# Gradient products of a trained layer: the derivative as stationary operand, tokens with a column of ones as moving operand

## The chip, the cores and the metric

The kernel runs on one core of one Trainium2 chip. The metric is the device time of one execution in microseconds; the kernel before takes 12997.07 us (median of three runs, 12996.37 to 12998.29).

## The reference, cut to what matters

Four layers follow each other on x of shape (8, 64, 64, 64): a selective-scan block with attention-like gates, a channel and position attention, a layer whose weights are trained inside the forward pass, and a second attention. Only the third is touched:

```python
def _modifier(params, x):
    w1, gn_w, gn_b, w2 = params
    h = jnp.einsum('bchw,oc->bohw', x, w1)          # 64 -> 128 channels
    ...                                             # group norm over 8 groups, per image
    h = _gelu(h)                                    # exact gelu
    return jnp.einsum('bohw,co->bchw', h, w2)       # 128 -> 64 channels
...
loss_fn = lambda ps: _surprise(_modifier(ps, feat) + feat, running_mean, running_var)
for _ in range(INNER_STEPS - 1):                    # two steps
    grads = jax.grad(loss_fn)(params)
    moms = ...
    params = ...
```

An image has 64 x 64 = 4096 tokens. For the gradients the kernel needs, for each image: the product of the output's derivative dy with the activations (64 x 128, summed over all images it is the gradient of w2), the product of the derivative t before the gelu with the tokens (128 x 64), and the sum of t over the tokens (128 numbers). From the last two it works out the gradients of w1 and of the norm's gain and bias.

## The kernel before

`modifier_and_attention` (L1803) builds a `Modifier`, calls `moments` once (L1819), and then twice `prepare`, `slope`, `gradients`, `update` (L1821 to L1825). `moments` (L1356) loads the images in pairs, subtracts each channel's mean and keeps the tokens transposed in `xT`, 128 tokens on the partitions, for every image and each of 32 groups of 128 tokens 64 channels. `slope` computes dy for all tokens.

`gradients` (L1535) is the stage of the change. It works on blocks of 512 tokens of a pair of images, eight blocks for a pair, four pairs, so 32 blocks in a pass. For a block n:

- `hidden` (L1553): eight products of 128 tokens each into two PSUM banks (L1562); ScalarE squares them, adds a tiny number and copies them (L1566, L1567, L1570).
- `factors` (L1576): ScalarE's gelu into `at` (L1580) and exponential into `t` (L1581), each after a load of its activation table[...].
- `remainder` (L1583), `invert` (L1591), `derive` (L1595): VectorE makes `half` (L1587) and, for each image, a reciprocal (L1593); GpSimd makes from them the gelu's derivative with three operations per image (L1596 to L1598).
- `back` (L1600): TensorE brings dy back through w2 and also transposes it, 192 columns, the two images in the upper and lower half of the array's rows (L1609).
- `keep_dy` (L1614): ScalarE copies the transposed dy out of PSUM (L1617).
- `apply` (L1619): VectorE multiplies the derivative with what came back (L1623). GpSimd adds the result to a running sum `run` over the blocks of the pair (L1629 for the first block, L1631 for the others).
- `sums` (L1633): for each of the four groups of 128 tokens and each image two products: dy (stationary, 64 columns) with the activations (128 moving columns) into the rows 0 to 63 of the image's PSUM bank `acc` (L1642), and the tokens (stationary, 64 columns) with t (128 moving columns) into the rows 64 to 127 (L1645). They add up in PSUM over the eight blocks.
- `collect` (L1650), after the last block of a pair: four products of `run` with a column of ones for each image (L1656), copies out of PSUM, w2's gradient added by VectorE (L1662, L1664), and a transposition of the tokens' product (L1667), so that `mom` gets 128 rows of 64 columns and, in column 64, the sum of t.

The order of all this is written by hand (L1670 to L1696, under `manual_schedule`), and every engine takes its instructions in that order. Iteration n issues `factors`, `invert` of image 0, `remainder` and `derive` of image 0 for block n + 1, `keep_dy` of n, `hidden` of n + 2, `apply` of n, `invert` and `derive` of image 1 for n + 1, `sums` of n, `back` of n + 1, and `collect` where a pair ends.

Buffers set who waits for whom. `at`, `t`, `e` and `h` have two buffers, so the gelu of block n + 2 waits until `sums` of block n has read `at`, and the exponential of n + 2 until all have read `t` of n. `half` and `dyT` have one. The PSUM banks of `hidden` are two, so its products for block n + 2 wait until VectorE has read those of n + 1 in `remainder`. The two pairs of banks of `back` are one block's, and `acc` has two banks, one for each image of the pair.

## Time and profile before

| | |
|---|---|
| median of three runs | 12997.07 us |
| the profiled execution | 12995.36 us |
| its span, first to last instruction | 12993.6 us |
| mean granted TensorE clock over the span | 0.926 |
| PE busy | 11161.9 us (86%) |
| DVE busy | 10881.6 us (84%) |
| ACT busy | 7717.6 us (59%) |
| POOL busy | 6754.4 us (52%) |
| first gradient pass, 9930 to 10300 us: PE, DVE, ACT, POOL busy | 254.28, 307.22, 286.15, 310.28 us |
| second pass, 10417 to 10785 us | 252.50, 306.03, 286.16, 310.25 us |

PE is TensorE's matmuls, PEld its weight loads, DVE VectorE, ACT ScalarE, POOL GpSimd. A line of the groups gives the source line, engine and operation, the tile written and those read, the shapes and the count; after the first bar the busy time and the mean duration in ns; after the second the idle time of the engine just before, with what ended it. A line of the waits gives who waited for whom, the sum in us, the times and the longest. A line of the windows gives the stretch in us from the span's start, its length, the busy time of each engine in it with the number of instructions, then the granted clock of TensorE as a share of full speed, and two numbers on DMA. The two gradient passes are some 700 us of the 12994; the rest is the scan, the attentions and the stages around them.

### The profile page before, as it was taken

Reading aid. Unit: us, or ns where it says so; the run is one execution under the profiler, and the core shown is the slowest. Engines: PE = TensorE matmul, PEld = TensorE weight load, DVE = VectorE, ACT = ScalarE, POOL = GpSimd, SP = SyncE. Lnnn points to the kernel's source line nnn. Section 1 sums busy time; section 2 is a strip of 40 time slices with the busy share of each in tenths; the row PEclk is TensorE's granted clock in tenths of the full one; section 3 lists DMA queues with packets and bytes.
Section 4 is the critical chain, followed back from the end, with each engine's and each line's share of the span. In section 5 each row is a group of like instructions: output and inputs, shape, how many; then the busy total and the mean of one; then the engine's idle time right before and its main releaser. Section 6 shows DMA issues by size and latency. Waiting matters only on the chain. (4 is left out here: it accounts for less than half of the span.)

```text
span 12993.6 us, 115955 instructions
## 1 busy us (share of the span) xinstructions
PE 11161.9 (86%) x36395; PEld 4115.1 (32%) x36395; DVE 10881.6 (84%) x7636; ACT 7717.6 (59%) x10047; POOL 6754.4 (52%) x3126
## 2 busy tenths in 40 slices
PE   7788888888888888888887779999996768999999
PEld 2233232232232232232232222323324553333332
DVE  5999999999999999999999958677686786766766
ACT  4676675675675666766765536445465674544544
POOL 4877888878888888788788830000003681000000
PEclk8999999999999999999999989999998888999999
DMA  4888888888889888888888830000001100000000
GB/s 164 301 292 291 308 301 293 306 298 303 300 300 309 296 296 308 300 298 305 297 299 304 295 120 6 24 18 11 17 6 66 39 27 23 6 16 17 6 10 6
DMA packets 686280, 2333.69 MB, mean 180 GB/s; under 512 B 98224, under 2 KB 98896, under 8 KB 683088
## 3 DMA queue, kind: packets, MB, share of 16 engines
q1 hardware_dynamic: 685648, 2326.13, 51.8%
q8 instruction: 290, 4.75, 0.1%
q14 instruction: 342, 2.80, 0.1%
HBM read 2240.69 MB, written 76.28 MB: 178 GB/s over the span
## 5 line engine op out<-in xcount | busy, mean ns | idle before, releaser
L614 POOL TENSOR_TENSOR ct<-ct,h 128x1024 f32<-128x1024 f32 x2048 | 4799.6, 2357 | 1447.1 <-DVE h L605 969.2
L642 PE MATMUL yps<-ct,ident 128*128 128x512 f32 x8192 | 4233.9, 652 | 547.3 <-POOL ct L614 545.3
L605 DVE TENSOR_TENSOR_SCAN h<-a,state,bdu 128x1024 f32<-128x1024 f32 x1344 | 3153.8, 2347 | 227.3 <-ACT state L609 26.7
L915 DVE TENSOR_TENSOR sum<-sum,ex 128x1024 f32<-128x1024 f32 x1920 | 2347.9, 1223 | 770.7 <-ACT ex L908 655.6
L908 ACT ACTIVATE ex<-sc 128x1024 f32<-128x1024 f32 x2048 | 1985.1, 1021 | 1529.8 <-PE sc L903 1529.7
L642 PEld LDWEIGHTS yps<-ct,ident 128*128 128x128 f32 x8192 | 1586.9, 205 | 3164.6 <-issue 1959.1
L582 ACT ACTIVATE a<-dt,amat 128x1024 f32<-128x1024 f32 x2048 | 2333.4, 1142 | 18.1 <-POOL dt L535 14.9
L601 DVE TENSOR_TENSOR bdu<-bt,du 128x1024 f32<-128x1024 f32 x1792 | 2194.9, 1225 | 101.4 <-ACT du L561 46.3
L922 PE MATMUL av<-ex,v 128*64 128x512 f32 x8192 | 1987.8, 606 | 0.0
L609 ACT COPY state<-h 128x1 f32<-128x1 f32 x2048 | 382.9, 187 | 2191.1 <-DVE h L605 2189.4
L903 PE MATMUL sc<-q,k 16*128 16x512 f32 (+1 forms) x8192 | 1656.3, 628 | 5.0 <-ACT ex L908 4.4
L605 DVE TENSOR_TENSOR_SCAN h<-a,bdu 128x1024 f32<-128x1024 f32 x448 | 1024.3, 2286 | 83.5 <-ACT state L609 16.7
L922 PEld LDWEIGHTS av<-ex,v 128*64 128x64 f32 x8192 | 498.2, 136 | 1363.9 <-issue 1360.5
L903 PEld LDWEIGHTS sc<-q,k 16*128 16x128 f32 (+1 forms) x8192 | 562.1, 184 | 1078.8 <-ACT ex L908 743.5
L1220 POOL TENSOR_TENSOR gt<-gt,pad 128x1024 f32<-128x1024 f32 x16 | 34.9, 2180 | 1617.5 <-ACT gt L1219 1538.1
L590 POOL TENSOR_TENSOR bt<-bt,dus 128x1024 f32<-128x1024 f32 x256 | 602.9, 2355 | 8.9 <-DMA bt<-bc 8.8
L408 PE MATMUL vps<-pad,convd 128*128 128x512 f32 x1152 | 534.2, 597 | 5.6 <-ACT z L393 5.6
L605 DVE TENSOR_TENSOR_SCAN h<-a,state,bt 128x1024 f32<-128x1024 f32 x192 | 499.5, 2602 | 15.0 <-POOL bt L590 8.2
L1593 DVE RECIPROCAL r<-e 128x512 f32<-128x512 f32 x128 | 420.7, 3323 | 0.0
L637 PE MATMUL yps<-y,ident 128*128 128x512 f32 x384 | 301.7, 917 | 115.6 <-ACT y L623 115.5
L1596 POOL TENSOR_TENSOR r<-r,half 128x512 f32<-128x512 f32 x128 | 162.7, 1271 | 360.9 <-issue 188.0
L582 ACT ACT_TABLE_LOAD x265 | 340.0, 1283 | 4.7
(402 smaller groups left out, 10325.1 us busy)
## 6 DMA issues: line engine op xcount, KB each, us to landing
bt<-bc SPq DMA_DIRECT2D x2048, 512.0 KB
ct<-bc SPq DMA_DIRECT2D x2048, 512.0 KB
x<-x SPq DMA_DIRECT2D x12, 2048.0 KB
bc<-e SPq DMA_DIRECT2D x256, 64.0 KB
zd<-z SPq DMA_DIRECT2D x64, 256.0 KB
z<-zd SPq DMA_DIRECT2D x64, 256.0 KB
x<-x SPq DMA_DIRECT2D x32, 512.0 KB
part<-x SPq DMA_DIRECT2D x128, 128.0 KB
```

The source lines that it names most:

```text
L408: nc.tensor.matmul(held[0].rearrange("p (r c) -> p r c", c=S), convd[:, t, :], pad[:, j * rows + dy : (j + 1) * rows + dy, dx : dx + S], s ...
L582: nc.scalar.activation(ctl["a", n], ctl["dt"], AF.Exp, scale=amat[:, ctl["k"], n : n + 1])
L590: nc.gpsimd.tensor_tensor(bt, bt, ctl["dus"], ALU.mult)
L601: nc.vector.tensor_tensor(z, bt, ctl["du"], ALU.mult)
L605: nc.vector.tensor_tensor_scan(h[:, flip], a[:, flip], z[:, flip], 0.0 if state is None else state[:, n : n + 1], ALU.mult, ALU.add,)
L614: nc.gpsimd.tensor_tensor(ct, ct, h, ALU.mult)
L642: nc.tensor.matmul(ctl["ps"][:, bass.ts(i, BK)], cm.ident, ct[:, bass.ts(i, BK)], start=False, stop=(n == N - 1),)
L903: nc.tensor.matmul(sc[:, e, :], k[r : r + d, bass.ts(j, 128)], qs[i][r : r + d, :], start=True, stop=True,)
L908: nc.scalar.activation(ex, sc, AF.Exp)
L915: nc.vector.tensor_tensor(sums[i], sums[i], ex, ALU.add)
L922: nc.tensor.matmul(avs[i][r, :], v[:, j, r], ex[:, e, :], start=(j == 0), stop=(j == TQ - 1))
L1593: nc.vector.reciprocal(r[n][s], e[n][:, s])
```

## The change

The token tile `xT` gets 65 columns instead of 64, the last of them filled with ones by VectorE. The second product of `sums` is turned round: t is the stationary operand (128 columns) and the tokens with their ones column move (65 columns), so that its result has 128 rows of 65 columns, in the orientation of `mom`, with the sum over the tokens in column 64. It now takes the columns 0 to 64 of the image's bank in all 128 rows; dy's product stands in the columns 128 to 255, image 0 in the rows 0 to 63, image 1 in the rows 64 to 127. Since the two products no longer share their start, each bank is opened with a product of zeros (one row, 128 columns stationary, 256 moving), and all others add to it. In each group of tokens the two dy products are issued first, then the two derivative products.

GpSimd's running sum goes, and with it in `collect` the products with the column of ones, the intermediate copies and the transpositions; ScalarE copies 128 x 65 numbers for each image. w2's gradient is gathered in a tile of 128 rows, one half for each image of the pair, and the halves are added after the last pair.

```diff
--- before.py
+++ after.py
@@ -1360,6 +1360,7 @@
         cm, nc, work = self.cm, self.cm.nc, self.work
         self.xc, self.pooled = self.kt([C + 1, NB, C], "xc"), self.kt([C, NB], "pooled")
         self.xT = tokens
+        self.cm.nc.vector.memset(tokens[:, :, :, C : C + 1], 1.0)
         cols = work.tile([2 * C, NB // 2], F32, name="mcols", tag="mcols")
         for p in range(NB // 2):
             x = self.load_pair(scratch[:, p, :], p, slice(0, L))
@@ -1381,7 +1382,7 @@
                         ps[:, i].rearrange("t b c -> t (b c)"), x[:, bass.ts(4 * j + i, 128)],
                         cm.ident,
                     )
-                dst = tokens[:, 2 * p : 2 * p + 2, 4 * j : 4 * j + 4, :]
+                dst = tokens[:, 2 * p : 2 * p + 2, 4 * j : 4 * j + 4, :C]
                 src = ps.rearrange("t q b c -> t b q c")
                 if j % 2:
                     nc.scalar.copy(dst, src)
@@ -1390,7 +1391,7 @@
             ps = self.bank("xxps")
             for q in range(TQ):
                 for e in range(2):
-                    t = tokens[:, 2 * p + e, q, :]
+                    t = tokens[:, 2 * p + e, q, :C]
                     nc.tensor.matmul(
                         ps[e * C : (e + 1) * C, :C], t, t, start=(q == 0), stop=(q == TQ - 1)
                     )
@@ -1539,7 +1540,10 @@
         cm, nc, work, p, g = self.cm, self.cm.nc, self.work, self.now, self.grad
         mom = self.kt([HID, NB, C + 1], "mom")
         blocks = [(pr, j) for pr in range(NB // 2) for j in range(NBK)]
-        at, t, h, e, r, half, hp, dyT, dp, acc, run = ({} for _ in range(11))
+        at, t, h, e, r, half, hp, dyT, dp, acc = ({} for _ in range(10))
+        w2 = work.tile([128, HID], F32, name="w2sum", tag="w2sum", bufs=1)
+        zero = work.tile([1, 2 * HID], F32, name="zero", tag="zero", bufs=1)
+        nc.vector.memset(zero, 0.0)
 
         def fetch(n):
 
@@ -1618,54 +1622,51 @@
 
         def apply(n):
 
-            pr, j = blocks[n]
             for s in range(2):
                 nc.vector.scalar_tensor_tensor(
                     t[n][:, s], t[n][:, s], 0.5, dp[n][s][:, :, :HID], ALU.add, ALU.mult
                 )
             dp.pop(n)
-            if j == 0:
-                run[pr] = work.tile([128, 2, 4, HID], F32, name="run", tag="run", bufs=1)
-                nc.gpsimd.tensor_copy(run[pr], t[n])
-            else:
-                nc.gpsimd.tensor_tensor(run[pr], run[pr], t[n], ALU.add)
 
         def sums(n):
+
 
             pr, j = blocks[n]
             if j == 0:
 
+
                 acc[pr] = [accs.tile([128, BK], F32, name="acc", tag="acc") for s in range(2)]
+                for ps in acc[pr]:
+                    nc.tensor.matmul(
+                        ps[:, : 2 * HID], zero[:, :HID], zero, start=True, stop=False
+                    )
             for i in range(4):
+                stop = j == NBK - 1 and i == 3
                 for s in range(2):
-                    flags = dict(start=(j == 0 and i == 0), stop=(j == NBK - 1 and i == 3))
                     nc.tensor.matmul(
-                        acc[pr][s][:C, :HID], dyT[n][:, s, i, :], at[n][:, s, i, :], **flags
-                    )
+                        acc[pr][s][s * C : (s + 1) * C, HID : 2 * HID], dyT[n][:, s, i, :],
+                        at[n][:, s, i, :], start=False, stop=False,
+                    )
+                for s in range(2):
                     nc.tensor.matmul(
-                        acc[pr][s][C:, :HID], self.xT[:, 2 * pr + s, 4 * j + i, :],
-                        t[n][:, s, i, :], **flags,
+                        acc[pr][s][:, : C + 1], t[n][:, s, i, :],
+                        self.xT[:, 2 * pr + s, 4 * j + i, :], start=False, stop=stop,
                     )
 
         def collect(pr):
 
-            momT = work.tile([128, 2, HID], F32, name="momT", tag="momT", bufs=1)
-            for s, ps in enumerate(acc[pr]):
-                b = 2 * pr + s
-                for i in range(4):
-                    nc.tensor.matmul(
-                        ps[:, HID : HID + 1], run[pr][:, s, i, :], cm.ones[:, 0:1],
-                        start=(i == 0), stop=(i == 3),
-                    )
-                nc.scalar.copy(momT[C:, s, :], ps[C:, :HID])
-                if b == 0:
-                    nc.vector.tensor_copy(g["w2"], ps[:C, :HID])
+            for s, ps in enumerate(acc.pop(pr)):
+                rows = slice(s * C, (s + 1) * C)
+                nc.scalar.copy(mom[:, 2 * pr + s, :], ps[:, : C + 1])
+                if pr == 0:
+                    nc.vector.tensor_copy(w2[rows], ps[rows, HID : 2 * HID])
                 else:
-                    nc.vector.tensor_tensor(g["w2"], g["w2"], ps[:C, :HID], ALU.add)
-                nc.scalar.copy(mom[:, b, C : C + 1], ps[:, HID : HID + 1])
-            for s, ps in enumerate(acc.pop(pr)):
-                nc.tensor.transpose(ps[:, 2 * HID : 2 * HID + C], momT[C:, s, :], cm.ident[C:, C:])
-                nc.scalar.copy(mom[:, 2 * pr + s, :C], ps[:, 2 * HID : 2 * HID + C])
+                    nc.vector.tensor_tensor(
+                        w2[rows], w2[rows], ps[rows, HID : 2 * HID], ALU.add
+                    )
+            if pr == NB // 2 - 1:
+                nc.vector.tensor_copy(g["w2"], w2[C:])
+                nc.vector.tensor_tensor(g["w2"], g["w2"], w2[:C], ALU.add)
 
         with self.cm.tc.manual_schedule():
             fetch(0)
@@ -1816,7 +1817,7 @@
             accs = train.enter_context(tc.tile_pool(name="t_acc", bufs=2, space=PSUM))
             mod.two = lambda: wide.tile([128, 2, BK], F32, name="hnps", tag="dps")
             ys = tok.tile([2 * C, NB // 2, L], F32, name="ys")
-            mod.moments(tok.tile([128, NB, TQ, C], F32, name="xT"), ys)
+            mod.moments(tok.tile([128, NB, TQ, C + 1], F32, name="xT"), ys)
             gs = mod.gates()
             for s in range(STEPS):
                 mod.prepare(wide)
```

## The prediction

> **What bounds the kernel now.** I read the page first (span, engines, slices), then the groups of the stretch 9900 to 10800 us, which holds both gradient passes, then the waits there, the timeline of a few blocks, and TensorE's clock in short windows.

> ```profile
> span 12993.6 us, 115955 instructions
> PEclk8999999999999999999999989999998888999999
> POOL 4877888878888888788788830000003681000000
> ```

> The page: slices 31 to 33 are the only ones in the second half in which GpSimd works and TensorE's granted clock drops; there lies the change. Groups of 9900 to 10800 us:

> ```profile
> L1593 DVE RECIPROCAL r<-e 128x512 f32<-128x512 f32 x128 | 420.7, 3323 | 0.0
> L1642 PE MATMUL acc<-at,dyT 128*64 128x128 f32 x1024 | 187.3, 344 | 9.5 <-ACT dyT L1617 9.5
> L1562 PE MATMUL htps<-hw,part 65*128 65x128 f32 x1024 | 186.8, 356 | 180.3 <-DVE half L1587 159.2 <-issue 21.1
> L1645 PE MATMUL acc<-t,xT 128*64 128x128 f32 x1024 | 180.4, 343 | 16.9 <-DVE t L1623 16.8
> L1596 POOL TENSOR_TENSOR r<-r,half 128x512 f32<-128x512 f32 x128 | 162.7, 1271 | 360.9 <-issue 188.0 <-DVE half L1587 163.5 <-DVE r L1593 9.3
> L1631 POOL TENSOR_TENSOR run<-run,t 128x1024 f32<-128x1024 f32 x56 | 132.3, 2363 | 1.6 <-DVE t L1623 1.6
> L1656 PE MATMUL acc<-ones,run 128*128 128x1 f32 x128 | 18.8, 277 | 1.6 <-POOL run L1631 1.6
> ```

> Each float32 product counts twice (x1024 for 64 blocks of 8). Waits of 9930 to 10800 us:

> ```profile
> ACT e L1566 <- PE htps L1562: 72.2, 58, 13.4
> DVE t L1623 <- ACT dyT L1617: 51.4, 38, 1.4
> ACT momT L1660 <- PE acc L1656: 32.2, 10, 8.4
> ACT L1580 <- PE acc L1645: 30.1, 30, 1.3
> ```

> In the timeline the first `half` (L1587) of a pass's block 0 and of its block 31 stand 327.7 us apart (9944.2, 10271.9; second pass 327.0): 31 intervals, 10.28 us each, or 13.3 where a `collect` lies in it. Per block GpSimd needs 10.16 (start to start of L1596, 10098.36 to 10108.52), VectorE 8.81 where it never idles (10094.80 to 10103.61), ScalarE 8.81. Two things hold the 10.28: GpSimd is full, and every second block TensorE is slow, so that ScalarE waits for it. The windows show the second:

> ```profile
> 10077.64:10081.05 3.41, 0.01 (x2) 0.00 (x0) 3.41 (x2) 3.37 (x4) 3.25 (x4) 1.00 0.00 0
> 10081.05:10084.47 3.42, 3.04 (x14) 3.04 (x15) 3.42 (x5) 1.97 (x5) 3.26 (x4) 0.50 0.00 0
> 10084.47:10087.88 3.41, 3.41 (x30) 3.19 (x31) 3.41 (x2) 2.69 (x5) 3.41 (x2) 0.50 0.36 81
> 10087.88:10091.29 3.41, 2.04 (x26) 1.57 (x22) 2.10 (x2) 2.76 (x3) 3.25 (x4) 1.00 0.00 1
> 10098.12:10101.53 3.41, 0.07 (x2) 0.00 (x0) 3.41 (x3) 3.37 (x4) 3.25 (x4) 1.00 0.00 0
> ```

> After the length come PE, PEld, DVE, ACT, POOL and the clock: an empty stretch of 3.41 us, then two at half clock, then full.

> **The change, part by part.** *Removed:* L1629/L1631, 140.6 us of GpSimd; it then needs about 8.0 a block and bounds nothing. Next is VectorE's 8.81.

> *TensorE's sums (L1642/L1645).* Before, the two products of an image sit side by side in 64 columns each: 16 steps of 0.109, 1.74 us. After, only the dyT products pair (8 steps, 0.87); the derivative is a 128-column weight, alone in the array, 16 steps that the load holds at 0.112 though only 65 columns move (1.79). And the mode changes 8 times within the sums instead of once, each 0.09 plus a slow second step of 0.05 to 0.10: 0.17, in all 1.36. Sums: 4.0 at full clock. The switch is the unknown: 0 if a load hides in it, 0.25 if it costs both slow steps in full; sums 2.7 to 4.7. At half clock 8 x 0.213 + 16 x 0.224 + 8 x 0.22 = 7.0.

> *The ring at full clock.* The next gelu into `at` waits for the last dyT product (release 0.24); then table and gelu 2.35, table and exponential 2.36, first dyT copy 0.31, two applies 1.28, and sums from the first derivative product to the last dyT one, 4.0 - 0.4 - 0.6 = 3.0: 9.5 us, over VectorE's 8.81. At half clock TensorE's own queue is longer: L1562 3.78 (the chain's pieces), sums 7.0, L1609 2.6, changes 0.2: 13.6.

> *Which clock.* At 9.5 TensorE works 1.9 + 4.0 + 1.5 and is idle 2.1. A window needs 0.38 x 3.413 = 1.30 us of streaming. One that holds the gap has 1.3 us of neighbours, L1609 (streams 1.28 in 1.5) and L1562 (65 rows count as 96: 1.28 in 1.9): at most 1.1. So it falls, as does one with 1.6 to 1.9 us of the gap; such windows begin over about 1.7 of the 3.41 us, one gap in two. Thin sums (1.7 streamed in 4.0) don't help. A half-clock block leaves no gap, and L1609 with L1562 behind it fills a window to 0.765, so it lasts about a block; the return comes at a window's end, often in the next block. Share f of half-clock blocks: from (1 - f)/2 = f a third, with the late return up to a half. I take 0.42: 0.58 x 9.5 + 0.42 x 13.6 = 11.2 a block.

> *Collect.* Before, 13.3 instead of 10.28, since L1656 waits for L1631 and ScalarE and VectorE for it. After, two copies of 65 columns (two of 0.22), two VectorE operations of 0.28 before the next reciprocal, and at the next block's start four steps of zero product of 256 columns (0.213, at half clock double): 0.9 to 1.7. I take 1.3, three times: 4.

> *End of a pass.* Before, 10271.9 to 10292.1. L1631 (2.35), L1656 (3.58 at half clock) and two transposes go; the derivative products after the last apply take about 6 instead of 3.2. Gain 2.5 (0 to 4).

> *Small.* Strided token copies (32 of 0.6), a memset of 256 columns, the zero memsets, two more operations on g["w2"]: between -1 and +2 us; I take 0. The scan and both attentions keep their instructions.

> *Sum.* A pass: 31 x 11.2 + 4 = 351.2 against 327.4: +23.8; less 2.5: +21.3. Twice: +43. The profiled execution took 12995.36 for a span of 12993.6; +43 is 13038, and the median lies 1.7 above it: 13040.

> **Rivals.** *The clock stays full.* Then 31 x 9.5 + 3 + 2 (cold start) = 299.5: -28, end -2.5, twice: 12936, faster. For it: GpSimd really is full before, and TensorE works more. Against: a gap of 2.1 cannot fill a window. It decides below f = 0.25. 13%. *The gap and the gain balance:* f = 0.25 gives 10.5 a block, 31 x 10.5 + 4 - 2.5 = 327: 12997; cheap switches (sums 2.7) end near here as well, as the ring falls to 8.9 but the gap grows to 2.7. 17%. *The clock locks at half:* 13.6 us is almost four windows (13.65), so a block may fall at the same place each time; f = 0.7: 12.4 a block, twice +57: 13112, or above. 9%. *The forecast,* f from 0.3 to 0.6, 13010 to 13085: 61%. That the sum does something else is excluded: column 64 of the product is the sum over tokens.

> **How the numbers follow.** About 0.2% (26 us) is what a measurement can tell from no change. Faster is the first rival and a little of the second: 0.15; same most of the second and the low end of the forecast: 0.19; slower 0.66. The range 12965 to 13110 leaves out the full-clock case and most of the lock.

> **What would show it.** Derivative products stepping 0.11 at full clock, sums near 4.0; blocks between 9.4 and 13.7 us in no fixed rhythm; mean clock near 0.75 over a pass's regular blocks (0.82 over 10036.68 to 10122.01 before); GpSimd idle 2 us a block; ScalarE's gelu waiting for the dyT products. Wrong if the windows stay at 1.00, if the sums take under 3 us, or if every block takes the same time.

## The result, and the profile after

| | before | after |
|---|---|---|
| median | 12996.72 us (4 runs, 12993.31 to 12998.29) | 13096.01 us (4 runs, 13084.72 to 13114.83) |
| profiled execution | 12995.36 us | 13114.83 us |
| first pass, `half` of block 0 to `half` of block 31 | 327.8 us | 388.6 us |
| second pass | 327.0 us | 387.9 us |
| last `half` to the next stage, each pass | 20.2, 20.2 us | 18.7, 19.7 us |
| mean clock in these two stretches | 0.81, 0.81 | 0.61, 0.61 |

The changed kernel is slower, by under one per cent but clear of noise: ratio 1.0080, 95% interval 1.0068 to 1.0092, 99 us by the medians. Its profiled execution is the longest of its four. The two loops account for all of the profiled pair's 119.5 us: 60.8 and 60.9 more, less 1.5 and 0.5 at their ends. The rest of the kernel is unchanged.

The page of the changed kernel, its span, TensorE's clock and GpSimd in 40 slices:

```profile
span 13113.1 us, 115634 instructions
POOL 4877888888888888888788710000004361000000
PEclk8999998999999999998999889999997668999999
```

In slices 31 to 34, which hold the gradient passes, GpSimd goes from 3, 6, 8 and 1 tenths to 4, 3, 6 and 1, and in slices 31 to 33 the clock from three times 8 to 7, 6 and 6. The groups of 9900 to 10900 us in the changed kernel (its L1597, L1566, L1646, L1651, L1600 are L1593, L1562, L1642, L1645, L1596 of before):

```profile
L1597 DVE RECIPROCAL r<-e 128x512 f32<-128x512 f32 x128 | 420.8, 3324 | 0.2
L1651 PE MATMUL acc<-xT,t 128*128 128x65 f32 x1024 | 256.9, 395 | 0.7 <-DVE t L1626 0.3
L1566 PE MATMUL htps<-hw,part 65*128 65x128 f32 x1024 | 209.0, 387 | 62.0 <-DVE half L1591 44.5 <-issue 17.5
L1600 POOL TENSOR_TENSOR r<-r,half 128x512 f32<-128x512 f32 x128 | 162.3, 1268 | 601.3 <-DVE half L1591 297.8 <-issue 184.0 <-DVE r L1597 119.5
L1646 PE MATMUL acc<-at,dyT 128*64 128x128 f32 x1024 | 161.7, 408 | 5.5 <-ACT dyT L1621 5.5
```

VectorE's and GpSimd's operations take what they took. L1566 is an instruction that the change doesn't touch, and yet its mean goes from 356 to 387 ns, and its idle time from 180.3 to 62.0 us: TensorE is slow more often and waits less. The waits of 9930 to 10860 us turn round accordingly:

```profile
ACT L1584 <- PE acc L1646: 160.4, 53, 5.4
DVE half L1591 <- ACT at L1584: 134.8, 41, 5.7
ACT e L1570 <- PE htps L1566: 70.1, 87, 14.4
ACT mom L1660 <- PE acc L1651: 17.8, 10, 5.5
```

Before, TensorE waited for `half`; now the gelu waits for TensorE's sums, 53 times in the 64 blocks, and VectorE for the gelu. In the traces of both kernels the granted clock is 1.00 or 0.50, and each record of it but the last lasts a whole number of 3.41 us (6.83, 10.24, 13.65 us and so on; 638 records before, 600 after). Ten windows of 3.41 us, in two stretches, show why it stays so (busy time of PE, PEld, DVE, ACT, POOL, then the clock):

```profile
10168.12:10171.54 3.42, 3.42 (x19) 2.98 (x18) 1.53 (x3) 3.39 (x5) 1.66 (x2) 0.50 0.00 0
10171.54:10174.95 3.41, 3.41 (x18) 2.86 (x17) 3.41 (x3) 2.48 (x4) 2.14 (x2) 0.50 0.13 38
10174.95:10178.36 3.41, 3.41 (x19) 2.51 (x18) 3.41 (x2) 1.12 (x3) 2.36 (x2) 0.50 0.15 38
10178.36:10181.78 3.42, 3.42 (x18) 2.85 (x19) 0.69 (x1) 2.31 (x2) 1.43 (x2) 0.50 0.00 0
10181.78:10185.19 3.41, 3.41 (x19) 2.97 (x18) 1.92 (x4) 2.99 (x5) 2.05 (x2) 0.50 0.00 0
...
10219.33:10222.74 3.41, 3.41 (x20) 3.12 (x20) 1.03 (x2) 3.38 (x3) 0.60 (x2) 0.50 0.00 0
10222.74:10226.15 3.41, 3.40 (x30) 2.74 (x28) 2.05 (x4) 3.37 (x7) 2.87 (x3) 1.00 0.16 32
10226.15:10229.57 3.42, 3.42 (x32) 2.70 (x34) 3.42 (x2) 2.93 (x5) 1.27 (x2) 1.00 0.13 44
10229.57:10232.98 3.41, 1.20 (x14) 0.91 (x11) 3.41 (x3) 3.37 (x4) 3.25 (x4) 1.00 0.00 0
10232.98:10236.39 3.41, 3.41 (x18) 3.19 (x19) 3.05 (x4) 2.26 (x6) 3.25 (x3) 0.50 0.10 24
```

At half clock PE is busy without a break, and VectorE and ScalarE have time to spare (in single windows they are busy for only 0.69 and 1.12 us). The clock stays at half for 68.27 us here (10154.47 to 10222.74), five blocks: one of 14.73, the first of a pair, and four of 13.27. It returns at 10222.74; the first gap, of 2.21 us, in the window at 10229.57, ends the full clock 10.24 us after the return. This pattern fills both passes: runs of one to five blocks at half clock, 13.27 us each (14.7 for the first of a pair), and between them a block of 10.33, often with one or two of 11.1 to 12.6, in which the clock changes. By the share that the prediction used (the part of a window in which TensorE streams, weighted by rows; that rows count in steps of 32 was the author's choice and is not shown), the windows at half clock from 10168.12 on read, in fours, one block or so to a row:

```
0.81 0.66 0.52 0.65
0.78 0.61 0.53 0.72
0.75 0.62 0.53 0.73
0.72 0.60 0.51 0.81 -> full clock
```

### The profile page after: what moved, and what is told of

Its sections match the earlier page's. It is cut to its first block, busy times and chain, and to the rows that moved or that the text cites. A ratio compares the mean times of both kernels' runs of the same rounds, so it can differ in the third digit from the quotient of the medians.

```text
span 13113.1 us, 115634 instructions
## 1 busy us (share of the span) xinstructions
PE 11427.6 (87%) x36283; PEld 4297.0 (33%) x36283; DVE 10887.3 (83%) x7643; ACT 7716.5 (59%) x10015; POOL 6618.2 (50%) x3062
## 3 DMA queue, kind: packets, MB, share of 16 engines
q1 hardware_dynamic: 685648, 2326.13, 51.4%
## 5 line engine op out<-in xcount | busy, mean ns | idle before, releaser
L605 DVE TENSOR_TENSOR_SCAN h<-a,state,bt 128x1024 f32<-128x1024 f32 x192 | 497.0, 2589 | 18.4 <-POOL bt L590 11.6
L1600 POOL TENSOR_TENSOR r<-r,half 128x512 f32<-128x512 f32 x128 | 162.3, 1268 | 601.3 <-DVE half L1591 297.8
L1597 DVE RECIPROCAL r<-e 128x512 f32<-128x512 f32 x128 | 420.8, 3324 | 0.2
```

The costliest lines, as they stand in the source:

```text
L605: nc.vector.tensor_tensor_scan(h[:, flip], a[:, flip], z[:, flip], 0.0 if state is None else state[:, n : n + 1], ALU.mult, ALU.add,)
L1597: nc.vector.reciprocal(r[n][s], e[n][:, s])
```

## The experiments

Theory A: the gap of 2.1 us makes the clock fall, the thin sums keep it from coming back, and TensorE at half clock is the bound. Thin are sums whose products stream for only a part of the time that they take, as the derivative products, where 65 columns move in a step of 0.112 us, as long as that of 128. Rivals: the switches (of the array between two 64-column products and one of 128) and the longer sums cost what was lost, at any clock (B); the weight of 128 columns itself (D); relief of GpSimd is worth nothing (E), or is a real gain that is merely outweighed (F). Each kernel ran beside the kernel before; ratios are to that. In the runs with products of zeros the tile of zeros has 128 rows.

**Filling the gap.** *First run*, with four products of zeros after `back` in all blocks but a pair's last:

```diff
+        def fill(n):
+            for i in range(4):
+                nc.tensor.matmul(acc[blocks[n][0]][0][:, 2 * HID :], zero[:, :HID], zero,
+                                 start=False, stop=False)
...
                         back(n + 1)
+                        if blocks[n][1] != NBK - 1:
+                            fill(n)
```

> The changed kernel, and after each block's back-products four more products of zeros with zeros (128 rows and columns, 256 moving columns, about 1.7 us at full clock) into unused columns of the accumulators, so that TensorE's gap of 2.1 us is filled; the sums are untouched. Theory A (the gap makes windows fall under 0.38, and TensorE at half clock is the bound): the windows stay at full clock, a block takes 9.3 to 9.6 us, a pass some 298 instead of 388 us, the kernel 12910 to 12945 us. Rival B (the longer sums and their mode switches cost what was lost, whatever the clock): TensorE gets 1.75 us more work a block, so the time stays at 13096 or rises, to 13200 us.

Measured: 12996.52 us, ratio 1.0000 (0.9991 to 1.0008), so 99 us under the changed kernel, with some 1.7 us more for TensorE to do in most blocks (an estimate: eight steps of 0.213, half of the 0.427 by which the 256 columns of L1640 step at half clock in the changed kernel). Rival B is out. The size was missed by 52 us: regular blocks take 9.26 and 9.59 us in turn, as theory A says, but not those at a pass's start and around a pair's end (10.65, 14.7, 11.2 to 11.9, 10.33), where nothing fills a gap of 3.4. Windows of this kernel, the regular stretch first:

```profile
9980.00:10020.00 40.00, 39.43 (x301) 31.66 (x299) 36.61 (x26) 37.23 (x51) 31.00 (x26) 1.00 0.10 27
10036.32:10039.74 3.42, 0.40 (x6) 0.10 (x2) 3.39 (x2) 3.38 (x4) 2.41 (x2) 1.00 0.00 0
10039.74:10056.81 17.07, 16.71 (x72) 13.18 (x73) 10.02 (x9) 9.87 (x15) 9.14 (x8) 0.50 0.07 16
```

One window with 0.40 us of TensorE in it, and 17 us at half clock follow: it is the fall of the changed kernel, alone and in one place.

*Second run*, with seven products at a pair's end as well:

```diff
+            for i in range(7 if last else 4):
...
                         back(n + 1)
+                        fill(n)
```

> The changed kernel with the products of zeros after every block's back-products, four in a pair's blocks and seven at its end, where the run before with four and none still fell to half clock (a gap of 3.35 us, then 17 us of half clock, in each of three places and at the start of a pass). Theory A: every block but the first two of a pass runs at full clock, 9.43 us, and 2 us more at a pair's end: 29 x 9.43 + 9.4 + 11 + 6 = 300 us a pass instead of 329, 12925 to 12955 us. Rival: the ends of the pairs cost 5 us or more each for another reason (copies, opening zeros), and the time stays at 12996 us.

Measured: 13024.27 us (1.0021, 1.0012 to 1.0031), a miss to the wrong side. ScalarE's timeline of this kernel at a pair's end:

```profile
10033.46 0.59 ACT L1574 COPY h<-htps 128x512 f32<-128x512 f32 x1
10039.94 0.33 ACT L1668 COPY mom<-acc 128x65 f32<-128x65 f32 x2 [5.90 <-PE acc L1659]
10040.29 1.28 ACT L1584 ACT_TABLE_LOAD   x1
```

The copies out of `acc` wait 5.90 us for the products of zeros (L1659), which were written into the same tile ahead of them, and the next gelu waits behind the copies. The edit cost what it should have saved.

*Third run*, the products at a pair's end issued after the copies:

```diff
+                    ps, last = acc[blocks[n][0]][0], blocks[n][1] == NBK - 1
+                    if last:
+                        collect(blocks[n][0])
+                    if n + 1 < len(blocks):
+                        fill(ps, last)
```

> The changed kernel with the products of zeros, those at a pair's end issued after the copies out of the accumulators; in the run with zeros everywhere the copies waited for them (10036.7 to 10039.9), and VectorE and ScalarE with the copies. Theory A: no gap at a pair's end, so no fall to half clock there: the extra of 7.9 us that each of three ends cost in the first run with zeros goes, a pass takes some 305 instead of 329 us, 12935 to 12965 us. Rival: the ends still fall to half clock, since the last sums of a pair and the first of the next are too thin: 12985 us or more.

Measured: 12976.59 us (0.9983, 0.9976 to 0.9990), 12 us over theory A's range and 8 under the rival's. Windows of this kernel at a pair's end:

```profile
10038.35:10041.76 3.41, 3.25 (x16) 2.60 (x15) 3.38 (x3) 3.38 (x4) 2.08 (x3) 1.00 0.00 0
10041.76:10045.18 3.42, 3.42 (x27) 2.73 (x26) 3.42 (x4) 2.93 (x7) 3.26 (x3) 1.00 0.22 61
10045.18:10055.42 10.24, 10.24 (x48) 7.98 (x48) 6.40 (x5) 6.30 (x9) 6.04 (x6) 0.50 0.03 7
```

The gap is gone, and the clock still falls, for 10.24 instead of 17.07 us: after a window in which PE is busy all the time, with products of 65 rows, the opening product of zeros of one row (L1640, 1.1 us) and the first thin sums. It happens at all three ends of both passes. So the rival named there is right in kind for the pairs' ends: here the fall came after thin work without a gap. What the window lacks is not settled by this run: by the prediction's share it reads 0.50, and in the changed kernel the window at 10226.15, at 0.51, kept the clock.

**Fewer switches.** The order within the sums altered:

```diff
             for i in range(4):
-                stop = j == NBK - 1 and i == 3
                 for s in range(2):
                     nc.tensor.matmul(acc[pr][s][s * C : (s + 1) * C, HID : 2 * HID], ...)
+            for i in range(4):
+                stop = j == NBK - 1 and i == 3
                 for s in range(2):
                     nc.tensor.matmul(acc[pr][s][:, : C + 1], ...)
```

> The changed kernel with the order within the sums altered: all dy products of a block first, then all derivative products, two mode switches in a block's sums instead of eight. Sums should take 3.0 us instead of 4.06 at full clock (six switches of 0.17 less) and 5.4 instead of 6.69 at half clock. Theory A (half-clock TensorE is the bound): half-clock blocks 12.0 instead of 13.27 us, full-clock ones 8.9, most blocks still at half clock, 12960 to 13040 us. Rival B (switches cost their full-clock 0.17 us each, 6 x 31 x 2 of them): 63 us less, 13033 us, with the half-clock share as before. Rival D (neither: what costs is the 128-column derivative itself): no change, 13096 us.

Measured: 12998.28 us (1.0000, 0.9992 to 1.0008), 98 us under the changed kernel, against 63 by rival B; rival D, which expected no change, is out as the whole cause. Blocks wholly at half clock take 12.46 us, not 12.0, and the mean clock of the passes is 0.69 and 0.67 instead of 0.61: still far from the 0.81 before, with the 128-column weight still there. The timeline of a block in this kernel at half clock, with one switch within the sums and 5.5 us from the first dy product to L1613:

```profile
10165.59 1.98 PE L1645 MATMUL acc<-at,dyT 128*64 128x128 f32 x16
10167.50 3.68 PE L1652 MATMUL acc<-xT,t 128*128 128x65 f32 x16
10171.11 1.33 PE L1613 MATMUL dps<-both,ys 64*128 64x192 f32 x6
```

With the products of zeros as in the second run above (the copies waiting, too):

> Both edits at once: dy products first in the sums, and the products of zeros after every block. Theory A with the ring: the gelu no longer waits for a product late in the sums, so VectorE's and ScalarE's 8.81 us set the block, some 8.95: 29 x 8.95 + 9.4 + 11 + 6 = 286 us a pass and a shorter end, 12890 to 12930 us. Rival (once the clock is full the mode switches are hidden): as with the zeros alone, 12925 to 12955 us.

Measured: 13004.99 us (1.0007, 0.9998 to 1.0015), 19 us less than the run with the change's order; both expectations were missed by the copies' wait (5.02 us at the first pair's end), so this run settles little. Repeated with the products after the copies:

> The same with dy products first in the sums (two mode switches for eight). Regular full-clock blocks were 8.81 and 9.41 us in turn with this order and 9.26 and 9.59 with the change's order, 0.31 us less in the mean: 9 us a pass, and 3 us less at its end, so 12905 to 12945 us and some 20 to 25 us under the run beside it. Rival (order matters only at half clock): within 10 us of the run beside it.

Measured: 12939.37 us (0.9953, 0.9939 to 0.9966), in the range, and 37 us under the run beside it where 20 to 25 were expected. The clock falls here too, in part at other places (after gaps of 1.62 us in the regular stretch), but its mean over the passes, 0.90 and 0.91, is that of the run beside it, 0.91. Order thus matters at full clock too, since the last dy product comes 2.4 us earlier in the sums (after 8 x 0.109 instead of 3.27 us, at 10228.15 in the changed kernel) and the gelu behind it: in the regular stretch blocks take 8.81 and 9.41, or 9.01 and 9.21 us.

**What GpSimd's relief is worth.** The running sum put back into the changed kernel:

```diff
             dp.pop(n)
+            if blocks[n][1] == 0:
+                run[0] = work.tile([128, 2, 4, HID], F32, name="run", tag="run", bufs=1)
+                nc.gpsimd.tensor_copy(run[0], t[n])
+            else:
+                nc.gpsimd.tensor_tensor(run[0], run[0], t[n], ALU.add)
...
```

> The changed kernel with GpSimd's running sum put back (its result is not used), and each bank opened with three narrower products of zeros, to save room. Theory A: GpSimd needs 10.16 us a block and TensorE 13.27 at half clock, so the sum is hidden in most blocks: 13085 to 13120 us. Rival F (the relief of GpSimd is a gain that the turned products merely outweigh): GpSimd full again costs as it did before, 13150 us or more.

Measured: 13124.14 us (1.0088, 1.0074 to 1.0102; the changed kernel 1.0068 to 1.0092), 4 us over theory A's range; the two can't be told apart, and F's 13150 is not reached. In this kernel GpSimd still waits for `half` (144 us in the two passes; 141.0 lie between them), which waits for the gelu, and that for TensorE:

```profile
POOL r L1599 <- DVE half L1590: 285.1, 49, 141.0
ACT L1583 <- PE acc L1652: 162.5, 53, 6.1
```

The other way round, the sum left out of the kernel before:

```diff
-            if j == 0:
-                run[pr] = work.tile(...)
-                nc.gpsimd.tensor_copy(run[pr], t[n])
-            else:
-                nc.gpsimd.tensor_tensor(run[pr], run[pr], t[n], ALU.add)
...
```

> The kernel before with GpSimd's running sum left out and nothing put in its place (the sum over the tokens isn't computed; ones stand for it). It tells what relieving GpSimd is worth when the products stay side by side. Theory A: VectorE's 8.81 us at full clock and TensorE's 9.9 at half clock take turns, about 9.4 us a block instead of 10.28, 12920 to 12945 us. Rival E (the relief is worth nothing, since shorter blocks only leave the clock lower): within 26 us of the kernel before, 12997 us.

Measured: 12962.55 us (0.9973, 0.9963 to 0.9984), between the two expectations: the relief is worth 35 us here. A pass is 11 us shorter, and 4.8 more at its end, but most blocks still take 10.33 and 10.2 us in turn. Windows of this kernel:

```profile
10008.47:10011.88 3.41, 0.06 (x2) 0.00 (x0) 3.41 (x3) 3.37 (x4) 3.15 (x3) 1.00 0.00 0
10011.88:10015.29 3.41, 2.98 (x14) 2.98 (x15) 3.41 (x5) 1.96 (x5) 3.25 (x4) 0.50 0.00 0
10015.29:10018.71 3.42, 3.42 (x30) 3.19 (x31) 3.42 (x2) 2.76 (x5) 2.44 (x2) 0.50 0.32 77
```

An empty window, two at half clock, three at full, as in the kernel before and with hardly a change in length: two blocks are six windows, 20.48 us. The clock holds this pace without GpSimd. Is GpSimd then no bound at all? Two runs with products of zeros in the gap, first with the sum, then without:

```diff
+                nc.tensor.matmul(acc[blocks[n][0]][0][:, 3 * HID :], zero, zero,
+                                 start=last, stop=last)
...
                         back(n + 1)
+                        fill(n)
```

> The kernel before with 14 products of zeros (128 rows, 128 columns, about 3.0 us at full clock) after each block's back-products. If GpSimd's 10.16 us a block hold the kernel before as much as the clock does: 12975 to 13000 us, since only the 0.12 us above 10.16 can go. Rival (the clock alone holds it, GpSimd has room): 9.3 us a block or less, 12930 us or less.

> The kernel before without GpSimd's running sum (the sum over the tokens isn't computed, ones stand for it) and with ten products of zeros (2.1 us) after each block's back-products. Without the sum alone the blocks still took 10.2 and 10.3 us in turn, half clock in every second one. Theory A (with GpSimd relieved the clock is what is left): 8.9 us a block, some 280 us a pass instead of 316, 12870 to 12910 us. Rival H (something else, such as ScalarE's chain, holds these blocks at 10.2 us): 12950 us or more.

Measured: 12991.73 us (0.9995, 0.9987 to 1.0003) with the sum, 12951.37 us (0.9965, 0.9951 to 0.9978) without. With it the later blocks of a pair take 10.18 us at full clock: GpSimd's 10.16, as expected. (A pair's end takes 15.5 instead of 13.3 us, since the products for the sum queue behind those of zeros, so the total hides part of what the earlier blocks gain.) Without the sum most blocks take 8.81 and 9.41 us. The total is 41 us over theory A's range and just inside H's; but H's reason, that something else holds these blocks at 10.2 us, is out by the blocks themselves. What is missing lies in single windows that still fall and in a pair's end of 13 us (as above, the copies wait for the products of zeros, 3.36 us at the first). So GpSimd and the clock were two bounds of nearly the same size in the kernel before: with either alone taken away most blocks stay at 10.2 us, with both they take 9.1.

**Side by side, with the sum on TensorE.** The operands are not turned. The orientation of before stays, and a third product is added, with ones as the weight and t moving, the two images in the two halves of the array's columns; ten products of zeros follow `back`, at a pair's end after the copies:

```diff
+                for s in range(2):
+                    nc.tensor.matmul(
+                        acc[pr][s][s * C : (s + 1) * C, HID : 2 * HID], cm.ones,
+                        t[n][:, s, i, :], start=False, stop=stop,
+                    )
...
+                nc.tensor.matmul(ps[:, 2 * HID + C : 2 * HID + C + 1], row[one, :],
+                                 cm.ones[one, 0:1], start=True, stop=True)
```

> The orientation of the kernel before (tokens stationary, all products side by side), with the sum over tokens taken from TensorE by a third product per image and group, 64 columns of ones stationary and t moving, side by side for the two images: eight steps of 0.109, 0.87 us a block, no mode switch. Ten products of zeros fill the gap, at a pair's end after the copies. Theory A: the block at full clock is as without any sum, 8.81 and 9.41 us in turn, TensorE thicker than there (the run without sum still had windows at half clock now and then): 12915 to 12955 us. Rival I (the 0.87 us lies on the ring and the ends of the pairs keep their transposes): 12965 us or more.

Measured: 12926.59 us (0.9943, 0.9930 to 0.9957), in theory A's range, so rival I is out. It is the fastest of all, and faster than both kernels, though it computes all that they compute. Most blocks take 8.81 and 9.41 us in turn, 10.6 to 10.8 where a `collect` lies in them; the mean clock is 0.96 and 0.97 in the passes. Without the products of zeros:

> The kernel with the third product (columns of ones stationary, everything side by side) without the products of zeros. TensorE has 0.87 us a block more to do at full clock than the kernel before, less than the changed kernel's 2.3 more, and its sums stream nearly all the time. Theory A (what locks the changed kernel at half clock is that its sums are thin: side by side they would bring a half-clock window to 0.765, and the clock back after two windows): half clock in two windows of six, blocks of 10.3 and 10.3 to 10.8 us in turn, 12965 to 13000 us. Rival J (any added work of TensorE at half clock makes the lock): runs of half-clock blocks of about 11.6 us, 13030 us or more.

Measured: 12990.78 us (0.9995, 0.9987 to 1.0004), in theory A's range; rival J is out. Windows of this kernel:

```profile
10078.49:10081.90 3.41, 3.35 (x32) 3.03 (x30) 3.41 (x2) 2.70 (x5) 1.44 (x2) 0.50 0.23 65
10081.90:10085.32 3.42, 2.55 (x34) 2.08 (x30) 3.42 (x3) 2.68 (x3) 3.01 (x3) 1.00 0.02 5
10085.32:10088.73 3.41, 2.69 (x22) 2.25 (x22) 2.13 (x4) 3.37 (x6) 3.20 (x3) 1.00 0.04 13
10088.73:10092.14 3.41, 3.29 (x34) 3.09 (x32) 3.41 (x2) 2.65 (x5) 1.37 (x2) 0.50 0.20 64
```

The clock falls here too, once in three windows where theory A had two in six, but after a single half-clock window, filled with products side by side (0.89 by the prediction's share), it is full again. The mean clock, 0.81, is that of the kernel before. The sum is off GpSimd here too, and the kernel takes 105 us less than the changed one. The added work is smaller than the change's, an estimated 0.87 us (eight steps of the 0.109 of before) against 2.3; but the 14 full-width products of zeros put into the gaps of the kernel before (an estimated 3.0 us, 28 steps of half the 0.213 that 128 columns take at half clock) made no lock either (mean clock 0.93 and 0.94).

## Why the prediction held, and where it was short

**The sign and the mechanism held**: the change is slower because TensorE is slowed to half clock more often and its queue then is the bound; filling the gap takes all of the loss away. The size was short, +43 us against +99 by the medians. That the median lies in the stated range, 14 us under its end, owes something to luck: it is 11 us over the forecast's own band of 13010 to 13085, and the profiled execution, 13114.83, lies outside the range.

**The sums.** Steps of 0.112 us, as predicted: with a weight of 128 columns a step takes that whether 1, 65 or 128 columns move (L1656 of before, L1651, L1566), so the columns that move don't set it; that the load does was the author's estimate. Four dy instructions in two steps, four derivative ones and two switches take 0.96 us at full clock, so the sums take 3.84, or 4.06 with a wait for t, against 4.0; at half clock 6.69 against 7.0. A switch is (0.96 - 2 x 0.109 - 4 x 0.112) / 2 = 0.15 us and not 0.17. The changed kernel's timeline at full clock:

```profile
10226.07 0.44 PE L1646 MATMUL acc<-at,dyT 128*64 128x128 f32 x4
10226.44 0.66 PE L1651 MATMUL acc<-xT,t 128*128 128x65 f32 x4
10227.02 0.44 PE L1646 MATMUL acc<-at,dyT 128*64 128x128 f32 x4
...
10228.94 1.57 PE L1613 MATMUL dps<-both,ys 64*128 64x192 f32 x16
10232.72 0.58 PE L1566 MATMUL htps<-hw,part 65*128 65x128 f32 x2 [2.21 <-DVE half L1591]
```

**The ring.** 9.5 us at full clock: 9.26 and 9.59 in the first run with zeros. Half-clock block 13.6: 13.27. Gap 2.1: most are 2.07 to 2.21. These held; the gap of 3.37 us after a pair's end was not in the prediction.

**Which clock: the step that failed in size.** "A half-clock block leaves no gap, and L1609 with L1562 behind it fills a window to 0.765, so it lasts about a block": the term was the share f of half-clock blocks, 0.42. From the pass of 388.6 us less the predicted 4 at the pairs' ends, a block has 12.4 us, so f = (12.4 - 9.5) / (13.27 - 9.5) = 0.77; by time the clock is at half 78% of a pass (0.61 = 1 - 0.78 / 2), where the prediction had a mean clock of 0.75. What failed is that one block is enough. The stretch L1613 and L1566 is 6.6 us long at half clock, but a window has to fall inside it, and in the run above the best window of a row reads 0.75 to 0.81, just at the bound: at 10168.12 a 0.81 stayed at half, at 10219.33 a 0.81 returned. Over both passes 13 windows of 0.77 to 0.82 stayed at half and 21 of 0.77 to 0.85 returned, so 0.765, read off the half-clock windows of the kernel before, was too low a bound here. A block of 13.27 us is 0.38 short of four windows, so the next chance comes in a slightly other place each time, and up to five blocks pass. That is the third rival, lock at half, with 13112 us: its reason (blocks fall in the same place for long) is half right, and its number is the profiled execution's. The other executions, down to 13084.72, lie between the forecast's 13040 and that.

**Removed work.** "Two things hold the 10.28" held in the sense that each alone gives 10.2: without the sum by the clock, at full clock by GpSimd. The prediction took from it, rightly, that GpSimd's relief would leave VectorE's 8.81 as the floor. The runs with zeros show that this is reached only with the clock up.

**Collect and end of pass.** A pair's end was put at 1.3 us: at full clock 10.65 against 9.43, so 1.2; at half clock one of them took 15.76 and the block after it 13.77. The ends gained 1.5 and 0.5 us and not 2.5. Small parts at 0: the rest of the kernel differs by -0.2 us (119.5 - 121.7 + 2.0).

## What to carry to other kernels

Count a product on TensorE twice: what it takes, and what it does to the clock. Here a weight of 128 columns for 65 moving ones, with a switch of the array's form between the products, made the sums 2.3 us longer at full clock, and in a loop with gaps the clock was back at full for less of the time (mean 0.61 instead of 0.81). How much of that is the thin products' and how much the switches' stays open: with two switches instead of eight the mean clock rose to 0.68 only, against 0.81 before. The same sum as one more product side by side was an estimated 0.87 us of work and left the clock at the 0.81 of before. Where two bounds are equal, relieving one gives only the difference to the other, so fill the gap (here with products of zeros, out of the way of anyone who waits for their tile) before judging what the relief is worth.

## What was not expected

- With products of zeros in the gap the clock stood at 1.00 over 40 us (9980.00 to 10020.00 in the first run with them).
- The loop keeps step with the windows of 3.41 us: two blocks in six windows before (20.5 us), one in three with the third product and no zeros (10.2 us), although the blocks of this kernel take 9.1 at full clock.
- The share of the prediction is no exact law. In the run with the third product and no zeros windows of 0.43 to 0.51 fell to half clock again and again, and in the run with dy first, of the windows at half clock that read as 0.8 or so, 19 stayed and 15 returned. What the clock follows stays open.
